# Gene products of two token tiles taken together: column groups shared by two tiles, and half of the array's rows for each tile's second product

## The chip, the cores and the metric

The kernel runs on one core of a Trainium2 chip. The metric is the device time of the whole program in microseconds, from a run of the core on the given inputs. Before the change three runs gave a median of 586.94 us (586.6 to 588.18).

## The reference

Two layers over x of 4 batches x 512 tokens x 256 features. Each layer normalises x and adds an attention-like part and a feed-forward part. The change lies in the feed-forward part of layer 0, which picks 32 of 512 "genes" for every token:

```python
logits = einsum('btd,gd->btg', xn, Wc) / clip(temperature, 0.1)
top_vals, top_idx = top_k(logits, 32)
expr_w = softmax(top_vals)
expressed = einsum('btk,btkc->btc', expr_w, genes[top_idx])     # 32 values a token
down = tanh(einsum('btc,dc->btd', expressed, Wd))
up = einsum('btc,dc->btd', expressed, Wu)
out = down * xn * up * scale
```

Beside it stands a linear attention with a running sum over the tokens. Layer 1 has another such attention (the "mixing"), a dense gated part, and 16 experts of which each token uses two.

## The kernel before

All is fp32. A tile is 128 tokens, a batch four tiles. The work runs in stages. In a stage the function `together` (L43) takes turns between generators: `layer0` (L224) of one batch or half batch, `mix` (L361) of the batch before it, and `dense` (L566), layer 1's dense part, a stretch of 11 chunks at a time, which has no other waits than its own and fills PE. The stages are L636 and L637 (batch 0 in two halves, so two tiles each), L643 to L645 (batches 1, 2 and 3 with four tiles each), and L673 on, where layer 0 is over. Then come routing, scatter, experts and the rest of the dense part. A scheduler puts the instructions of a stage in order on each engine, by what depends on what and in the order of the turns; each engine then runs its own list strictly from the front.

For one tile `layer0` does this. `logits` (L286) multiplies with Wc into a PSUM bank and ScalarE copies it out (L293). `top` (L296) is eight passes over 512 values on VectorE (L301, L302) and one product (L309) that leaves the unnormalised weights e of the 32 chosen genes, zero elsewhere, and the reciprocal rden of their sum. In between, a share of the attention is done (`attend_kv`, `attend_q`, L244 to L280). Then `express` (L313):

- four transposes turn e into one PSUM bank (L316), ScalarE copies it to wT (L318);
- four products with the genes, 128 rows and 32 columns each, one for each chunk of 128 genes (L321). Each writes 32 other partitions of one bank, so each lies in another column group of the array. The four partial sums are not added here: ScalarE copies all 128 partitions to exT (L322);
- one product of exT with wdut (L324) over 128 rows. wdut holds Wd and Wu side by side, repeated four times over the partitions (L126), so that this product adds the four partial sums too. Its 512 columns fill a bank;
- Tanh on ScalarE (L326), a small and a large product on VectorE (L328, L329), and on POOL four operations (L331 to L334) that put the result into xs.

After the tiles, `out` (L336) multiplies the attention with Wo, and VectorE adds it to xs (L342). In the next stage `mix` takes the statistics of xs. Its ScalarE part copies q and k (L391), takes squares (L396), a square root (L405, with a table load) and eight exponentials (L410, L411); its VectorE part has running sums (L421), a small softmax and top two for the router (L439 to L456). The dense part has pairs of products (L576), Tanh (L580), VectorE (L582), a copy (L586) and the products back (L596).

All layer 0 and mixing products take their PSUM bank from one pool of four (`bank`, L188). The tile pool of layer 0 (`io`) has two buffers of each name.

Of the kernel before, what the change touches and what calls it, by code (L numbers as in the profile page):

```python
# [11 lines left out]
F32 = mybir.dt.float32  # L12
# [4 lines left out]
P = 128  # L17
B, L, D = 4, 512, 256
NT = L // P
NH = D // P  # L20
NG, GD, NACT = 512, 32, 32
NGC = NG // P
# [31 lines left out]
def tile_two_layers(  # L54
# [24 lines left out]
    V, S, G, T = nc.vector, nc.scalar, nc.gpsimd, nc.tensor  # L79
# [41 lines left out]
    gn = wp.tile([P, NGC, GD], F32, name="gn")  # L121
    nc.sync.dma_start(gn, genes.rearrange("(c p) k -> p c k", p=P))

    wdut = wp.tile([P, 2 * D], F32, name="wdut")
# [60 lines left out]
    io = first.enter_context(tc.tile_pool(name="io0", bufs=2, side="right"))  # L185
    one = first.enter_context(tc.tile_pool(name="one0", bufs=1, side="right"))

    def bank():  # L188
        return ps_m.tile([P, L], F32, name="pm")
# [4 lines left out]
    def statistics(pool, b, i0, nt):  # L194

        mv = pool.tile([P, NT, 2], F32, name="mv")
        rs = pool.tile([P, 2, NT], F32, name="rs")
        ve = pool.tile([P, NT], F32, name="ve")
        for i in range(nt):
            bs = pool.tile([P, 6], F32, name="bs")  # L200
            V.bn_stats(bs, xs[:, b, i0 + i])
            V.bn_aggr(mv[:, i], bs)
        V.tensor_scalar(rs[:, 0, 0:nt], mv[:, 0:nt, 1], LN_EPS, None, ALU.add)
        V.reciprocal(ve[:, 0:nt], rs[:, 0, 0:nt])
        V.tensor_tensor(ve[:, 0:nt], ve[:, 0:nt], mv[:, 0:nt, 1], ALU.mult)
        V.tensor_scalar(rs[:, 1, 0:nt], ve[:, 0:nt], RMS_EPS, None, ALU.add)
        S.activation(rs[:, :, 0:nt], rs[:, :, 0:nt], AF.Sqrt)
        V.reciprocal(rs[:, :, 0:nt], rs[:, :, 0:nt])
        return mv, rs

    def normalise(to, b, i0, nt, mv, rs):
        for i in range(nt):
            V.tensor_scalar(
                to[:, i], xs[:, b, i0 + i], mv[:, i, 0:1], rs[:, 0, i : i + 1], ALU.subtract, ALU.mult
            )
# [8 lines left out]
    def layer0(b, i0, nt):  # L224

        W = nt * P
        mv, rs = statistics(io, b, i0, nt)
        xn = io.tile([P, NT, D], F32, name="xn")
        normalise(xn, b, i0, nt, mv, rs)

        sl = io.tile([P, 2, NT], F32, name="sl")
        V.tensor_scalar(sl[:, 0, 0:nt], rs[:, 1, 0:nt], rtemp, None, ALU.mult)
        V.tensor_scalar(sl[:, 1, 0:nt], rs[:, 1, 0:nt], scl, None, ALU.mult)
        yield
        xnT = io.tile([P, NH, L], F32, name="xnT")
        for h in range(NH):
            S.copy(xnT[:, h, 0:W], turn(xn, nt, h * P))
        yield


        def project(c):
            pm = bank()[:, 0:W]
            for h in range(NH):
                T.matmul(  # L244
                    pm,
                    wqkv[:, h, c * P : (c + 1) * P],
                    xnT[:, h, 0:W],
                    start=(h == 0),
                    stop=(h == NH - 1),
                )  # L250
            return pm

        def phi(c):

            pm = project(c)
            e = io.tile([P, L], F32, name="phi", bufs=3)[:, 0:W]
            S.activation(e, pm, AF.Relu, bias=nbqk[:, c : c + 1], scale=-1.0)
            S.activation(e, e, AF.Exp, scale=-1.0)
            V.scalar_tensor_tensor(e, pm, bqkv1[:, c : c + 1], e, ALU.add, ALU.max)
            return e  # L260

        ctxT = one.tile([P, NH, L], F32, name="ctxT")
        cums = {}

        def attend_kv(h):
            fk = phi(2 + h)
            pv = project(4 + h)
            kv = one.tile([P, L], F32, name="kv")[:, 0:W]
            V.scalar_tensor_tensor(kv, pv, bqkv[:, 4 + h : 5 + h], fk, ALU.add, ALU.mult)
            cum = io.tile([P, L], F32, name="cum")[:, 0:W]  # L270
            V.tensor_tensor_scan(
                cum, ones[:, 0:W], kv, carry[:, h : h + 1] if i0 else 0.0, ALU.mult, ALU.add
            )
            if i0 + nt < NT:
                V.tensor_copy(carry[:, h : h + 1], cum[:, W - 1 : W])
            cums[h] = cum

        def attend_q(h):
            fq = phi(h)
            V.scalar_tensor_tensor(ctxT[:, h, 0:W], fq, QSCALE, cums[h], ALU.mult, ALU.mult)  # L280


        rden = io.tile([P, NT], F32, name="rden")
        exT = one.tile([P, L], F32, name="exT")

        def logits(i):  # L286
            pl = bank()
            for h in range(NH):
                T.matmul(  # L289
                    pl, xnT[:, h, i * P : (i + 1) * P], wct[:, h], start=(h == 0), stop=(h == NH - 1)  # L290
                )
            lg = io.tile([P, NG], F32, name="lg")
            S.copy(lg, pl)  # L293
            return lg

        def top(i, lg):  # L296
            tp = io.tile([P, NACT], F32, name="top")
            rep = io.tile([P, NG], F32, name="rep")
            for r in range(NACT // 8):
                src = lg if r == 0 else rep  # L300
                V.max(tp[:, 8 * r : 8 * r + 8], src)  # L301
                V.match_replace(rep, tp[:, 8 * r : 8 * r + 8], src, TAKEN)  # L302
                if r == 0:
                    nm = io.tile([P, 1], F32, name="nm")
                    V.tensor_scalar(nm, tp[:, 0:1], sl[:, 0, i : i + 1], -1.0, ALU.mult, ALU.mult)
                    e = io.tile([P, NG], F32, name="e")
                    S.activation(e, lg, AF.Exp, bias=nm, scale=sl[:, 0, i : i + 1])
            den = io.tile([P, 1], F32, name="den")
            V.scalar_tensor_tensor(e, rep, TAKEN, e, ALU.is_equal, ALU.mult, accum_out=den)  # L309
            V.reciprocal(rden[:, i : i + 1], den)  # L310
            return e

        def express(i, e):  # L313
            pw = bank()
            for c in range(NGC):
                T.transpose(pw[:, c * P : (c + 1) * P], e[:, c * P : (c + 1) * P], ident)  # L316
            wT = io.tile([P, NGC, P], F32, name="wT")
            S.copy(wT.rearrange("p c t -> p (c t)"), pw)  # L318
            px = bank()
            for c in range(NGC):  # L320
                T.matmul(px[c * GD : (c + 1) * GD, 0:P], gn[:, c], wT[:, c], start=True, stop=True)  # L321
            S.copy(exT[:, i * P : (i + 1) * P], px[:, 0:P])  # L322
            du = bank()
            T.matmul(du, exT[:, i * P : (i + 1) * P], wdut, start=True, stop=True)  # L324
            dn = io.tile([P, D], F32, name="dn")
            S.activation(dn, du[:, 0:D], AF.Tanh, scale=rden[:, i : i + 1])  # L326
            cf = io.tile([P, 1], F32, name="cf")
            V.tensor_tensor(cf, rden[:, i : i + 1], sl[:, 1, i : i + 1], ALU.mult)  # L328
            V.scalar_tensor_tensor(dn, du[:, D : 2 * D], cf, dn, ALU.mult, ALU.mult)  # L329
            xw = io.tile([P, D], F32, name="xw")  # L330
            G.tensor_tensor(xw, xn[:, i], nwb, ALU.mult)  # L331
            G.tensor_tensor(dn, dn, xw, ALU.mult)
            G.tensor_tensor(xs[:, b, i0 + i], xs[:, b, i0 + i], bob, ALU.add)
            G.tensor_tensor(xs[:, b, i0 + i], xs[:, b, i0 + i], dn, ALU.add)  # L334

        def out(i):  # L336
            ao = bank()[:, 0:D]
            for h in range(NH):
                T.matmul(  # L339
                    ao, ctxT[:, h, i * P : (i + 1) * P], wot[:, h], start=(h == 0), stop=(h == NH - 1)  # L340
                )
            V.tensor_tensor(xs[:, b, i0 + i], ao, xs[:, b, i0 + i], ALU.add)  # L342


        parts = [lambda h=h, f=f: f(h) for h in range(NH) for f in (attend_kv, attend_q)]
        lg = logits(0)
        for i in range(nt):
            nxt = logits(i + 1) if i + 1 < nt else None
            e = top(i, lg)
            yield  # L350
            for part in parts[i * len(parts) // nt : (i + 1) * len(parts) // nt]:
                part()
            yield
            express(i, e)
            lg = nxt
            yield
        for i in range(nt):
            out(i)
            yield
# [270 lines left out]
    def a(b, i0, nt):  # L630
        return layer0(b, i0, nt), 2 + 4 * nt
# [170 lines left out]
    for step, _ in enumerate(dd):  # L802
# [11 lines left out]
        while added < 2 * NTT and 17 * added <= 32 * (step - 3):  # L814
# [4 lines left out]
            if added % 4 == 0 and added < 2 * NTT:  # L819
                b, i = divmod(n - 1, NT)  # L820
# [55 lines left out]
```

## Time and profile before

| | |
|---|---|
| runs, median (lowest to highest) | 586.94 us (586.6 to 588.18) |
| the profiled execution | 591.42 us |
| its span, first to last instruction | 589.7 us |
| mean granted TensorE clock | 0.975 |
| busy: PE, weight loads, DVE, ACT, POOL | 539.4, 393.0, 373.1, 232.6, 173.9 us |
| L321, 128 passes on PE | 7.0 us busy, 293 ns each |
| L324, 32 passes on PE | 17.8 us busy, 639 ns each |
| L318 and L322, 16 copies each on ACT | 9.2 and 4.2 us |
| L301 and L302, 64 each on DVE | 43.9 and 43.2 us |

PE is TensorE's products, DVE VectorE, ACT ScalarE, POOL GpSimd. Busy time of PE counts each pass to its modelled end, and passes overlap: a pass of 512 columns is listed with 592 ns, yet the next one starts 0.43 us later. So the starts, not the lengths, tell what a product costs. The chain of waits is followed back from the last instruction: for each step, what released it.

### The profile page before, as it was taken

What the parts mean: (1) busy time and instruction counts of PE and PEld (TensorE: products, weight loads), DVE (VectorE), ACT (ScalarE), POOL (GpSimd) and SP (SyncE); (2) the same over time, 40 slices, a digit from 0 to 9 for tenths busy, and PEclk for the clock granted to TensorE, in tenths of its full rate; (3) what the DMA queues carried; (4) which work ended last, traced back from release to release, by engine and by line L of the source; (5) the groups of instructions that cost most, each with busy time, mean ns of one, the idle gap of its engine ahead of it and who ended that gap; (6) DMA issues with size and microseconds to landing.
All of it is one profiled execution on the core that took longest, in us unless ns stands there. A gap on an engine that the chain in (4) does not pass through costs nothing.

```text
span 589.7 us, 7350 instructions
## 1 busy us (share of the span) xinstructions
PE 539.4 (91%) x2384; PEld 393.0 (67%) x2384; DVE 373.1 (63%) x992; ACT 232.6 (39%) x528; POOL 173.9 (29%) x214
## 2 busy tenths in 40 slices
PE   3557989989999999999999999969999999999987
PEld 1334656558565685656877778857777777788876
DVE  3979999997896797967943785322222222235563
ACT  1453746653555625556265311103333333321111
POOL 1234232353221432224440326661000000006651
PEclk9788999999999999999999999989999999999999
DMA  4993000000000000000075602224233333114441
GB/s 159 375 377 140 1 1 1 2 0 1 1 1 0 1 1 1 1 1 1 1 236 170 182 2 80 91 86 136 90 108 107 108 108 98 55 63 125 126 133 46
DMA packets 38453, 47.39 MB, mean 80 GB/s; under 512 B 4016, under 2 KB 34960, under 8 KB 38160
## 3 DMA queue, kind: packets, MB, share of 16 engines
q1 hardware_dynamic: 35344, 38.53, 20.0%
q0 software_dynamic: 3072, 8.39, 4.6%
q8 instruction: 20, 0.33, 0.2%
q14 instruction: 17, 0.14, 0.1%
HBM read 28.30 MB, written 18.61 MB: 80 GB/s over the span
## 4 chain that ended last, share of the span: by engine, by line
PE 61%; DVE 21%; ACT 6%; POOL 4%; issue 3%; DMA 2%; SPq 0%; another core or an unknown queue 0%; POOLq 0%; ACTq 0%; DVEq 0%
PE gu L576 16%; PE pu L740 9%; PE acc L596 9%; PE py L761 7%; PE pm L384 5%; DVE rep L302 4%; DVE top L301 4%; PE pt L703 3%; POOL xrows L544 3%; PE pm L244 3%; PE pm L289 2%; PE pm L221 2%; PE pm L339 2%; DVE sums L430 2%; DVE sums L421 1%
## 5 line engine op out<-in xcount | busy, mean ns | idle before, releaser
L576 PE MATMUL gu<-yT,wugt 128*128 128x256 f32 x512 | 127.5, 385 | 0.0
L576 PEld LDWEIGHTS gu<-yT,wugt 128*128 128x128 f32 x512 | 96.0, 192 | 19.5 <-issue 7.2
L580 ACT ACTIVATE th<-gu 128x256 f32<-128x256 f32 (+1 forms) x88 | 33.0, 382 | 133.4 <-PE gu L576 85.9
L806 POOL DMA_INDIRECT ys<-yrows,slot x32 | 30.7, 961 | 145.4 <-PE gu L576 130.1
L596 PE MATMUL acc<-wot,hid 128*128 128x256 f32 x256 | 67.4, 386 | 5.9 <-DVE hid L584 5.5
L582 DVE SCALAR_TENSOR_TENSOR th<-th,gu 128x256 f32<-128x256 f32 (+1 forms) x88 | 36.1, 412 | 55.0 <-ACT th L580 46.3
L740 PE MATMUL pu<-wex,xgT 128*128 x188 | 63.8, 461 | 0.8 <-DMA xg<-xrows 0.8
L587 POOL TENSOR_TENSOR hid<-hid,th 128x256 f32<-128x256 f32 (+1 forms) x44 | 34.3, 782 | 101.1 <-ACT hid L586 97.8
L596 PEld LDWEIGHTS acc<-wot,hid 128*128 128x128 f32 x256 | 48.4, 192 | 15.5 <-DVE hid L584 5.9
L244 PE MATMUL pm<-xnT,wqkv 128*128 128x512 f32 (+1 forms) x120 | 46.7, 529 | 4.1 <-ACT lg L293 1.8
L576 PE MATMUL gu<-xn1T,sgu 128*128 128x256 f32 (+1 forms) x192 | 47.3, 382 | 1.4 <-ACT hid L586 1.3
L749 DVE TENSOR_TENSOR hb<-pu,hb 128x176 f32<-128x176 f32 x47 | 16.1, 342 | 51.0 <-ACT hb L748 51.0
L384 PE MATMUL pm<-w,xn1T 128*128 128x512 f32 (+1 forms) x128 | 45.7, 501 | 0.0
L761 PE MATMUL py<-wex,hgT 128*128 x188 | 44.5, 379 | 0.0
L761 PEld LDWEIGHTS py<-wex,hgT 128*128 128x128 f32 x188 | 35.6, 190 | 8.6 <-issue 0.2
L576 PEld LDWEIGHTS gu<-xn1T,sgu 128*128 128x128 f32 (+1 forms) x192 | 33.8, 181 | 9.5 <-ACT hid L586 2.6
L740 PEld LDWEIGHTS pu<-wex,xgT 128*128 128x128 f32 x188 | 32.0, 190 | 11.0 <-ACT xgT L717 1.0
L384 PEld LDWEIGHTS pm<-w,xn1T 128*128 128x128 f32 x128 | 24.6, 193 | 21.4 <-issue 17.9
L244 PEld LDWEIGHTS pm<-xnT,wqkv 128*128 128x128 f32 x120 | 23.8, 202 | 22.0 <-issue 13.2
L753 DVE COPY hgT<-pt 128x512 f32<-128x512 f32 (+1 forms) x24 | 16.3, 681 | 34.2 <-PE pt L703 34.2
L544 POOL DMA_INDIRECT xrows<-xn,slot x32 | 31.0, 969 | 23.8 <-DVE cpair L538 9.9
L301 DVE MAX8 top<-rep 128x8 f32<-128x512 f32 x48 | 32.9, 686 | 0.4
(162 smaller groups left out, 881.5 us busy)
## 6 DMA issues: line engine op xcount, KB each, us to landing
xrows<-zero SPq DMA_DIRECT2D x1, 6016.0 KB, 22.6
xg<-xrows SPq DMA_DIRECT2D x23, 256.0 KB, 2.7
yrows<-yg SPq DMA_DIRECT2D x23, 256.0 KB, 2.1
wex<-in_w_gate_up_dram SPq DMA_DIRECT2D x8, 704.0 KB, 4.8
xs<-in_x_dram SPq DMA_DIRECT2D x4, 512.0 KB, 7.7
wugt<-in_wug_dram SPq DMA_DIRECT2D x1, 2048.0 KB, 12.3
wex<-in_w_down_dram SPq DMA_DIRECT2D x4, 512.0 KB
out_dram<-xs SPq DMA_DIRECT2D x7, 256.0 KB, 2.7
```

What stands on the lines that cost most here:

```text
L244: T.matmul(pm, wqkv[:, h, c * P : (c + 1) * P], xnT[:, h, 0:W], start=(h == 0), stop=(h == NH - 1),)
L301: V.max(tp[:, 8 * r : 8 * r + 8], src)
L384: T.matmul(o[:, 0:n], xnT[:, h, i * P : (i + 1) * P], w1[:, h, at : at + n], start=(h == 0), stop=(h == NH - 1),)
L544: sc = G.indirect_dma_start(out=xrows, out_offset=bass.IndirectOffsetOnAxis(ap=slot[:, k, i : i + 1], axis=0), in_=xn1[:, i // NT, i % NT] ...
L576: T.matmul(gu[0:m, k], w[:, h, at : at + m], ins[which][:, h], start=(h == 0), stop=(h == NH - 1))
L580: S.activation(th[0:m], gu[0:m, 0], AF.Tanh, scale=0.5)
L582: V.scalar_tensor_tensor(th[0:m], th[0:m], 1.0, gu[0:m, 0], ALU.add, ALU.mult)
L587: G.tensor_tensor(hid[0:m], hid[0:m], th[0:m], ALU.mult)
L596: mm = T.matmul(acc[:, t], hid[0:m, t * P : (t + 1) * P], dw[0:m, dc], start=(n == 0 and t == 0), stop=(n == NC - 1), skip_group_check=True,)
L740: T.matmul(pg[:, 0 : 2 * NI], xT[:, i, h], wex[:, bass.ds(at[i] + h * 2 * NI, 2 * NI)], start=(h == 0), stop=(h == NH - 1),)
L761: mm = T.matmul(py[:, i * D : (i + 1) * D], hT[:, i, h], wex[:, bass.ds(at[i] + EW - (2 - h) * D, D)], start=(h == 0), stop=(h == 1),)
L806: G.indirect_dma_start(out=ys[:, asked], out_offset=None, in_=yrows, in_offset=bass.IndirectOffsetOnAxis(ap=slot[:, k, n : n + 1], axis=0) ...
```

## The change

`express` is split. `turn_genes` keeps the transposes and the copy to wT. A tile's wT is kept until the next tile has its own; then one `express` serves both tiles:

- the four column groups hold two tiles, two groups each. A tile's four chunks of 128 genes go into its two groups, two chunks added up in each. These are eight products for two tiles, as before;
- one copy of 128 partitions to exT for both tiles: the lower 64 belong to the first, the upper 64 to the second;
- the second product of each tile takes 64 rows, the lower or the upper half of the array, into a bank of its own;
- the rest, now `expressed`, is done for one tile and then the other.

```diff
-        exT = one.tile([P, L], F32, name="exT")
...
-        def express(i, e):
+        def turn_genes(e):
             pw = bank()
             for c in range(NGC):
                 T.transpose(pw[:, c * P : (c + 1) * P], e[:, c * P : (c + 1) * P], ident)
             wT = io.tile([P, NGC, P], F32, name="wT")
             S.copy(wT.rearrange("p c t -> p (c t)"), pw)
+            return wT
+
+        def express(i, wTs):
             px = bank()
-            for c in range(NGC):
-                T.matmul(px[c * GD : (c + 1) * GD, 0:P], gn[:, c], wT[:, c], start=True, stop=True)
-            S.copy(exT[:, i * P : (i + 1) * P], px[:, 0:P])
-            du = bank()
-            T.matmul(du, exT[:, i * P : (i + 1) * P], wdut, start=True, stop=True)
+            for c in range(2):
+                for g in range(NGC):
+                    j = g % 2 * 2 + c
+                    T.matmul(
+                        px[g * GD : (g + 1) * GD, 0:P], gn[:, j], wTs[g // 2][:, j], start=(c == 0), stop=(c == 1)
+                    )
+            exT = io.tile([P, P], F32, name="exT")
+            S.copy(exT, px[:, 0:P])
+            dus = [bank(), bank()]
+            for t, du in enumerate(dus):
+                half = slice(t * P // 2, (t + 1) * P // 2)
+                T.matmul(du, exT[half], wdut[half], start=True, stop=True)
+            for t, du in enumerate(dus):
+                expressed(i + t, du)
+
+        def expressed(i, du):
             dn = io.tile([P, D], F32, name="dn")
...
         lg = logits(0)
+        wTs = []
         for i in range(nt):
             nxt = logits(i + 1) if i + 1 < nt else None
             e = top(i, lg)
...
-            express(i, e)
+            wTs.append(turn_genes(e))
+            if len(wTs) == 2:
+                express(i - 1, wTs)
+                wTs = []
             lg = nxt
             yield
```

In the changed kernel's numbering the transposes are L315, the copy L317, the first products L327, exT L331, the second products L335, Tanh L341, and L595 is the dense L576.

## The prediction

> **What bounds the kernel now.** I read the page's row of slices first, then the busy time by stage, then the chain of waits from 250 us, then single instructions around the gene products. The first stages last until about 290 us; a 75 us stage is one batch of four tiles, with dense chunks as filler.
>
> Slices of the page (14.7 us each) and the stage 215 to 290 us (columns: window and length, then busy time and count by engine):
>
> ```profile
> PE   3557989989999999999999999969999999999987
> DVE  3979999997896797967943785322222222235563
> ...
> 215.00:290.00 75.00, 72.51 (x317) 48.50 (x316) 63.31 (x161) 39.77 (x89) 21.88 (x26) 1.00 0.00 1
> ```
>
> PE is busy 72.5 of 75 us, DVE 63.3. Until 90 us DVE is the full one (39.6 of 40 us from 50 to 90); after 290 us the edit touches nothing. But who ends last changes inside the stage. The chain (start, length, what):
>
> ```profile
> 250.42 0.34 DVE th L582
> ...
> 251.16 0.50 ACT wT L318
> 251.66 0.04 issue
> 251.70 0.43 PE pm L321 x8
> 252.13 0.63 PE gu L576 x2
> 252.76 0.88 PE pm L324 x2
> ...
> 261.92 1.73 PE pm L244 x4
> 263.65 0.02 issue
> 263.67 0.69 ACT phi L257
> ...
> 270.04 0.15 ACT exT L322
> ...
> 271.85 0.47 ACT dn L326
> ...
> 273.03 0.42 DVE th L582
> ...
> 275.67 1.14 DVE sums L421
> 276.81 0.04 issue
> 276.86 0.66 PE pm L316 x4
> ```
>
> So: VectorE from 223 to 251 us (the top-32 search, no gap over 0.15 us between 227 and 253), PE to 263.7, ScalarE to 273, VectorE to 276.8, then PE to the next batch. From this a saved PE microsecond counts only between 251.7 and 263.7 and after 276.8. The last two lines say why PE stood idle 1.37 us at 275.4: the transposes of tile 3's e wait for a PSUM bank that the scan frees.
>
> Now the edited products themselves, for one tile (start, busy):
>
> ```profile
> 251.70 0.43 PE L321 MATMUL pm<-wT,gn 128*32 128x128 f32 x8
> ...
> 252.06 0.70 PE L576 MATMUL gu<-yT,wugt 128*128 128x256 f32 x2
> ...
> 252.59 1.04 PE L324 MATMUL pm<-wdut,exT 128*128 128x512 f32 x2
> ```
>
> An fp32 product is two passes here. The eight passes of L321 in four column groups start at 251.70 and the next full-array pass at 252.06: 0.36 us, where two passes of 128 columns one after the other take 0.21 (L289 streams 512 columns in 0.43, so 128 take 0.107). So the four groups do run side by side, and 0.15 us goes to draining. The pair behind is 0.70 us busy instead of the usual 0.59: 0.1 more, weights that could not be loaded ahead.
>
> **What the skill says.** "TensorEngine Tiling (Array Packing)", Key Properties: tiles work independently, but changing the tiling mode drains the array; the 0.15 + 0.1 us above agree. "TensorE: Matmul & The Clock Gate", Part 3, Measured speedup: row groups overlap like column groups, 4 tiles of K=32, N=512 gave 3.07 times. No row group appears in this trace; the column groups agree in kind. The same page, Part 3, What overlaps: matmuls start and end in program order. Whether that holds up the second tile behind the first tile's second fp32 pass, no run here shows. "TensorEngine Tiling", Gotcha 1: row tiles need different PSUM banks; the edit takes two.
>
> **The change, part by part.**
>
> *1. First product.* Still eight passes per tile. Before, a tile costs 0.36 + 0.10 = 0.46 us of PE. After, a pair in one piece is 4 x 0.107 + 0.25 = 0.68. But the changed program's instruction order splits it in five of eight pairs: the first tile's two products, a dense product, the other six. That is 0.46 + 0.68 = 1.14 against 0.92 before. The first two wait for nothing new and lie in the wait for wT.
>
> *2. Second product.* Before 2 x 0.438 (mean slot of L324 from start to next start) = 0.88 per tile, 1.75 per pair. After, if both row groups overlap fully, 2 x 0.427 = 0.85, plus a drain 0.15 and weights exposed before and after, 0.1 to 0.2: 1.15. Bounds: 0.95 (everything hidden); 1.55 if only the middle passes overlap (3 x 0.427 + 0.25); 2.05 to 2.5 with no overlap (1.75 + 0.3, or each load exposed too). I take 1.15: the column groups in fp32 show full overlap and use the same hardware.
>
> *3. Copies.* One exT copy (0.27 us, 0.15 on the chain) per pair goes. Two Tanh (0.47 each), two products with cf (0.47), and their POOL work stay, in a burst at the second tile.
>
> *4. What moves.* The even tile's products leave their place. What that gives, stage by stage:
>
> Stage 215 to 290. (a) One dn (0.47 busy, 0.39 on the chain) leaves the full VectorE run: -0.4 at wT. PE's 1.3 us for the even tile leave that run too, and buy nothing: PE just waits longer for wT. (b) From wT to the first mixing products: before 251.70 to 253.64 = 1.94; after 0.68 + 0.43 + 1.15 = 2.26, so +0.3; and one dense pair of passes now stands behind instead of ahead, +0.4. At 263.7 that is -0.4 + 0.3 + 0.4 = +0.3. (c) In ScalarE's run the third tile's exT and dn go, 0.27 + 0.47: -0.4 at the last exp. (d) At 273 the router's small operations (L445 to L455, 2.2 us) stand ahead of the scan. In the changed order the router's Exp comes ahead of phi's, so they can run during ScalarE's eight exps. From the end of phi's Exp (267.8) VectorE still has 0.65 phi, 0.41 th, 0.74 kv, 0.3 small, 1.21 cum, 0.71 replace, 0.66 chosen = 4.7, until 272.5; then th 0.42 and the scan 1.14, until 274.1; 0.6 more for gaps and the later start: 274.7 instead of 276.8, -2.1 at L316. PE can follow: of the way there it was idle 1.37, and tile 2's products (1.34) are gone. (e) Last pair: before 276.86 to the out products at 281.54; after, 0.68 + 1.15 against one tile's 1.34, +0.5. Stage: **-1.6**.
>
> Stage 140 to 215: same order, but VectorE had a 0.51 us gap at 168.6 where PE was late, and the even tile's products lie in PE's own stretch; so (a) is -0.4 - 0.5 = -0.9, the rest as above: **-2.1**.
>
> Stage 90 to 140: VectorE is full but for 0.85 us at 103.9, where logits wait behind tile 0's products; that goes, -0.8, and a dn, -0.4; the last pair costs +0.5: **-0.7**.
>
> 50 to 90: VectorE full, its work unchanged. The two tiles' POOL work (0.73 + 1.3 each) now comes in one burst before the sums of L342: **+0.3**, bounds 0 and +1. It is hidden later: with four tiles POOL ended at 286 and the out sums are at 291.
>
> Start: the six projections of the second half waited behind tile 0's products, 25.1 to 28.7 us; VectorE has 3 us of idle there, but POOL still adds the tiles one by one: **-0.5**, bounds -1.5 and +1 (PE's clock was 0.79 here, and longer gaps may keep it low).
>
> Waits added: tile 1's bank. PE stops there with dense work queued behind it; four banks turn over, the pair holds px and then two. I take 0 and bound it by the longest wait PE had for a bank, 1.5 us per stage at worst.
>
> Sum: -0.5 + 0.3 - 0.7 - 2.1 - 1.6 = **-4.6 us**. The profiled execution took 591.42, its span 589.7 and 1.7 around; it would give 586.8. The median of the runs is 4.5 us lower than this execution. I apply the difference as it is: 586.94 - 4.6 = **582.3 us**.
>
> **Rivals.**
> *Absorbed.* (c) and (d) do not come, since PE or another ScalarE wait is late next. For it: PE is 97% busy, and only 1.37 us were idle. Then stages 4 and 5 give about -0.5 each: -0.5 + 0.3 - 0.7 - 1.0 = -1.9, and with partial overlap (1.55) back some 1 to 2 us: **586.0**.
> *Slower: the row tiles run one after the other.* Two fp32 passes of tile 0 go first in order, tile 1's behind them, and each half loads its weights exposed. A pair then takes 2.3 (between 2.05 and 2.5), 1.15 more, in about seven pairs that lie on PE's path: +8.0 - 4.6 = +3.4, **590.4**. For it: no row tile in the trace, and each half has its own semaphore. Against: the column groups overlap in the same two passes. It decides from 2.05 us per pair on: (2.05 - 1.15) x 7 = 6.3, which is the 4.6 gained and 1.8 more.
> *The change isn't what it says*: the order keeps pairs but the dense products between them force full-array mode each time. That is in the 1.14 above; for all eight pairs it adds 3 x 0.46 = 1.4: 583.7.
>
> **How the numbers follow.** Forecast with its last variant 0.55, absorbed 0.23, slower 0.22. A difference under 0.3% (1.8 us) cannot be told from none. The forecast is faster, up to its low end: a pair at 0.95 saves 8 x 0.2 = 1.6, the start another 1: 579.5. Absorbed lies from 584 to 587.5, half of it within 0.3%, a third faster; the serial case from 588 to 591.5, mostly slower. Range 579.5 to 590: it leaves out the tail of the serial case. Faster 0.59, same 0.19, slower 0.22.
>
> **What would show it.** Right: L335's four passes start in two waves 0.43 us apart and the next full-array pass 1.0 to 1.2 us after the first; PE idle before the last pair's transposes (1.37 us) shrinks; the stages get 1.5 to 2 us shorter each. Wrong: four starts 0.43 us apart (no overlap), or PE waits on L335 for VectorE (bank). Wrong in (d) if the scan still starts 3 us after the last exp. A stage that stays 75 us long with a PE that idles more is "absorbed".

## The result, and the profile after

Six runs of each kernel gave a median of 587.06 us before (586.12 to 588.18) and **583.53 us** after (582.32 to 585.08): a ratio of 0.9943, 95% interval 0.9928 to 0.9958, so 3.4 us faster. The profiled execution after took 584.1 us, its span is 582.3 us, the mean granted clock 0.981.

The two profiled spans differ by 7.4 us, more than the timed 3.4: from the first to the last scatter the kernel before took 43.9 us and the changed one 39.4. Over all profiles this length goes with the chip and not with the edit: about 44 us on the two chips on which the kernel before took 591 us, 39.4 on the two on which it took 587, for single products (even_twice below) and paired ones alike. It would also explain why the profiled execution before was 4.5 us above its median. I therefore compare stretches that end before the scatter, and timed runs.

The page's slices after, 14.6 us each; PE is at eight tenths or more from about 58 us on, but for two slices:

```profile
PE   3637989989999999999999989997999999999997
DVE  3969999998896897968943686331222222225563
```

And the stage from 215 to 290 us (window and length, then busy time and count of PE, weight loads, DVE, ACT, POOL):

```profile
215.00:290.00 75.00, 73.55 (x325) 49.66 (x324) 63.95 (x167) 39.65 (x88) 22.47 (x27) 1.00 0.00 1
```

In a fixed window PE is 1.0 us busier, though each pair now takes less of it: the stage has become shorter and more of the next work falls into the window (325 passes instead of 317). So a busy sum over a fixed window says nothing here; places in the stage have to be compared.

The chain of waits after, same stage (start, length, what):

```profile
247.25 0.34 DVE th L601
...
247.98 0.50 ACT wT L317
...
248.52 0.63 PE pm L327 x12
249.15 0.63 PE gu L595 x2
249.78 1.06 PE pm L335 x4
250.84 2.83 PE pm L403 x8
...
270.52 0.45 PE pm L221 x4
...
270.99 1.23 DVE sums L440
```

Before, ScalarE was on this chain from 263.7 to 273 us and VectorE to 276.8. Now PE is on it all the way from 248.5 to 271 us, and only the scan (L440) stands between that and tile 3's transpositions. Those single instructions, PE only (start, busy, and in brackets the idle time before and what ended it), first the transposition before the change and then the changed kernel:

```profile
276.86 0.33 PE L316 MATMUL pm<-ident,e 128*128 128x128 f32 x1 [1.21 <-DVE sums L421]
```

```profile
272.27 0.66 PE L315 MATMUL pm<-ident,e 128*128 128x128 f32 x4 [0.44 <-DVE sums L440]
...
273.73 0.50 PE L327 MATMUL pm<-wT,gn 128*32 128x128 f32 x8
274.16 0.70 PE L595 MATMUL gu<-yT,wugt 128*128 128x256 f32 x2
274.79 1.13 PE L335 MATMUL pm<-wdut,exT 64*128 64x512 f32 x4
275.85 1.13 PE L595 MATMUL gu<-yT,wugt 128*128 128x256 f32 x4
```

The idle time before the transpositions fell from 1.21 to 0.44 us. The four passes of L335 occupy PE from 274.79 to 275.85, 1.06 us for two tiles. In the single records they start at 274.790, 274.797, 275.323 and 275.330: two waves 0.53 us apart, both row tiles within 7 ns. The dense pass ahead of them is followed after 0.31 us instead of the usual 0.22 (both from the single records), so a pair takes 0.09 us more than its own 1.06. PE never waited on L335 for a bank; its only wait there is ScalarE's exT.

Where in the stage the time went. All are starts on PE after the stage's start, which I set at the end of the last addition of `out` (L342, L357 after) of the batch before (the last mixing ends with its last yT); stage 140 to 215 us:

| us from the stage's start | before | changed | same rows | delay only | router first | four together |
|---|---|---|---|---|---|---|
| tile 1's transpositions | 32.36 | 30.56 | 30.56 | 30.56 | 32.36 | 30.56 |
| first mixing product behind them | 35.53 | 34.71 | 35.57 | 35.47 | 35.53 | 31.00 |
| tile 2's transpositions | 49.84 | 49.54 | 50.41 | 49.77 | 49.83 | 46.60 |
| tile 3's transpositions | 58.92 | 56.20 | 57.07 | 56.71 | 57.99 | 53.53 |
| first `out` product | 63.44 | 61.61 | 63.33 | 62.70 | 62.51 | 61.60 |
| end | 75.20 | 73.18 | 74.05 | 73.87 | 74.26 | 75.18 |

The stage after it shows the same differences within 0.3 us (0.6 with four together), but for some ends. The last four columns are experiments. And the lengths of all stages, from the same ends:

| kernel | stage 2 (two tiles) | 3 | 4 | 5 | 6 (last mixing) |
|---|---|---|---|---|---|
| before | 44.5 | 59.0 | 75.2 | 75.1 | 49.8 |
| changed | 43.5 | 59.7 | 73.2 | 73.5 | 50.8 |
| same rows | 43.5 | 60.1 | 74.1 | 74.1 | 51.4 |
| delay only | 43.9 | 58.7 | 73.9 | 76.6 | 49.4 |
| router first, in the kernel before | 44.0 | 60.4 | 74.2 | 74.2 | 49.6 |
| router first, in the changed kernel | 43.6 | 60.3 | 73.9 | 74.1 | 50.3 |
| one piece | 42.8 | 58.9 | 73.2 | 75.7 | 49.4 |
| even tiles' product twice | 43.6 | 62.1 | 76.1 | 75.9 | 49.8 |
| stage 3 single | 43.7 | 60.6 | 73.2 | 73.2 | 50.8 |
| batch 0 single | 44.2 | 64.0 | 73.2 | 73.2 | 50.8 |
| four together | 43.3 | 62.7 | 75.2 | 74.5 | 53.6 |

### The profile page after: what moved, and what is told of

It reads as the page before. It is cut to its first block, busy times and chain, and to the rows that moved or that the text cites. A ratio compares the mean times of both kernels' runs of the same rounds, so it can differ in the third digit from the quotient of the medians.

```text
span 582.3 us, 7339 instructions
## 1 busy us (share of the span) xinstructions
PE 535.6 (92%) x2384; PEld 391.5 (67%) x2384; DVE 371.6 (64%) x992; ACT 231.4 (40%) x520; POOL 169.6 (29%) x214
## 4 chain that ended last, share of the span: by engine, by line
PE 51%; DVE 28%; POOL 7%; issue 6%; ACT 4%; DMA 4%; SPq 0%; POOLq 0%; ACTq 0%; DVEq 0%
PE gu L595 11%; PE pu L759 10%; PE py L780 7%; PE acc L615 6%; DVE rep L301 5%; DVE top L300 5%; PE pm L403 4%; PE pt L722 4%; POOL ys L825 3%; DVE sums L449 3%; POOL xrows L563 2%; DVE sums L440 2%; PE pm L244 2%; PE pm L221 2%; PE pm L288 2%
## 5 line engine op out<-in xcount | busy, mean ns | idle before, releaser
L595 PE MATMUL gu<-yT,wugt 128*128 128x256 f32 x512 | 125.4, 382 | 0.0
L595 PEld LDWEIGHTS gu<-yT,wugt 128*128 128x128 f32 x512 | 95.0, 190 | 20.4 <-issue 8.8
L615 PE MATMUL acc<-wot,hid 128*128 128x256 f32 x256 | 66.0, 381 | 0.4
L759 PE MATMUL pu<-wex,xgT 128*128 x188 | 65.1, 468 | 0.8 <-ACT xgT L736 0.8
L601 DVE SCALAR_TENSOR_TENSOR th<-th,gu 128x256 f32<-128x256 f32 (+1 forms) x88 | 36.6, 417 | 44.0 <-ACT th L599 43.7
L606 POOL TENSOR_TENSOR hid<-hid,th 128x256 f32<-128x256 f32 (+1 forms) x44 | 33.1, 756 | 101.9 <-ACT hid L605 96.0
L595 PE MATMUL gu<-xn1T,sgu 128*128 128x256 f32 (+1 forms) x192 | 46.9, 381 | 1.4 <-ACT hid L605 1.3
L780 PE MATMUL py<-wex,hgT 128*128 x188 | 44.5, 379 | 0.0
L595 PEld LDWEIGHTS gu<-xn1T,sgu 128*128 128x128 f32 (+1 forms) x192 | 34.0, 182 | 9.5 <-ACT hid L605 2.6
L605 ACT COPY hid<-gu 128x256 f32<-128x256 f32 (+1 forms) x44 | 16.4, 373 | 43.1 <-DVE th L601 42.9
```

The source lines that it names most:

```text
L595: T.matmul(gu[0:m, k], w[:, h, at : at + m], ins[which][:, h], start=(h == 0), stop=(h == NH - 1))
L601: V.scalar_tensor_tensor(th[0:m], th[0:m], 1.0, gu[0:m, 0], ALU.add, ALU.mult)
L606: G.tensor_tensor(hid[0:m], hid[0:m], th[0:m], ALU.mult)
L615: mm = T.matmul(acc[:, t], hid[0:m, t * P : (t + 1) * P], dw[0:m, dc], start=(n == 0 and t == 0), stop=(n == NC - 1), skip_group_check=True,)
L759: T.matmul(pg[:, 0 : 2 * NI], xT[:, i, h], wex[:, bass.ds(at[i] + h * 2 * NI, 2 * NI)], start=(h == 0), stop=(h == NH - 1),)
L780: mm = T.matmul(py[:, i * D : (i + 1) * D], hT[:, i, h], wex[:, bass.ds(at[i] + EW - (2 - h) * D, D)], start=(h == 0), stop=(h == 1),)
```

## The experiments

Each kernel was timed in five rounds beside the kernel before on the same chip; a ratio is to that.

**Does the overlap make the gain? (same_rows)** The changed kernel, with both second products on the lower 64 rows, so that they cannot lie side by side.

```diff
-            exT = io.tile([P, P], F32, name="exT")
-            S.copy(exT, px[:, 0:P])
+            exT = io.tile([P // 2, 2, P], F32, name="exT")
+            for t in range(2):
+                S.copy(exT[:, t], px[t * P // 2 : (t + 1) * P // 2, 0:P])
...
-                T.matmul(du, exT[half], wdut[half], start=True, stop=True)
+                T.matmul(du, exT[:, t], wdut[0 : P // 2], start=True, stop=True)
```

> The changed kernel, but both second products of a pair take the lower 64 rows (the second tile's half is copied down; one small copy more a pair), so that they cannot overlap; order on the engines nearly the same. Theory (the pairs lie in stretches where the array is late, and only the overlap pays for the pairing): a pair takes 1.95 us instead of 1.06, in six to seven of eight pairs on the path, +5.5 to +6.5: about 589.5 us, above the kernel before. Rival (the gain comes from the even tile's work leaving its place and from the new order of the router's operations, array time is hidden): within 1.5 us of the changed kernel, about 584.5.

Measured 1.0005 (0.9990 to 1.0019). PE in the trace of this kernel:

```profile
201.51 1.98 PE L335 MATMUL pm<-wdut,exT 64*128 64x512 f32 x4
203.42 1.13 PE L595 MATMUL gu<-yT,wugt 128*128 128x256 f32 x4
```

From start to next start 1.91 us instead of 1.06. In the table each pair puts this kernel 0.86 us further behind the changed one, 1.72 at the first `out` product. That is the array time alone: the second exT copy, which this kernel has besides, adds nothing at these places. So with both products on the same rows nothing of the gain is left, and the overlap is worth 0.62% of 587 us, 3.6 us against these. That lies between the 5.5 to 6.5 us of the theory and the 1.5 of the rival. The saved array time itself is larger: summed over stages 2 to 5, second products take 7.4 us in the changed kernel and 13.4 here. About 0.6 of a saved microsecond arrives at the end (0.4 to 0.8 by the intervals of the two ratios); the stage's end already shows 0.87 of the 1.72.

**Is the gain in the later place alone? (delay_only)** The kernel before, each tile with its own products as before, but both done at the second tile.

```diff
-            express(i, e)
+            wTs.append(turn_genes(e))
+            if len(wTs) == 2:
+                express(i - 1, wTs[0])
+                express(i, wTs[1])
+                wTs = []
```

> The kernel before, with its own products (four column groups and 128 rows for each tile), but both tiles' products stand at the second tile. Theory: the delay without the overlap puts an even tile's 1.3 us into the array's stretches and takes less than that from the others: 586 to 589 us, no gain. Rival (the delay is the gain): 583.5.

Measured 0.9979 (0.9966 to 0.9993): 1.2 us faster, a third of the gain. The table shows its way: tile 1's transpositions come 1.8 us earlier, which the first mixing product loses again (35.47 against 35.53), tile 3's come 2.2 us earlier, of which the last pair's products give back 1.5. The later place lets things start earlier; the overlap keeps the bill small. The other two thirds, about 2 us, come with the rest of the edit, the products that overlap.

**Is it the router's place? (before_router, after_router)** The router's largest value, Exp, sum and reciprocal written ahead of the square root in `mix`, once in each kernel.

```diff
+        V.tensor_reduce(mx, lg, AX.X, ALU.max)
...
+        S.activation(ee[:, :, 0:NE], ee[:, :, 0:NE], AF.Exp)
...
+        V.reciprocal(den, den)
         cf = w2.tile([P, 2, NT], F32, name="cf1")
```

> The kernel before, with the first half of the router's work (maximum, Exp, sum, product) written ahead of the square root of the mixing, nothing else changed. Theory (the router's small operations ahead of the scan held up the array 2 us in each of two stages): -2 to -4 us, 583 to 585. Rival (the change gained by array time alone; this order is worth nothing): 586.5 to 587.5.

> The changed kernel with the same edit of the router. Theory (the changed kernel's order already has this): within 1.5 us of the changed kernel, 582.5 to 585. Rival (the two add up): 580.

Measured 0.9985 (0.9968 to 1.0001) in the kernel before, whose chain now reads:

```profile
274.64 1.23 DVE sums L432
...
275.92 0.66 PE pm L316 x4
```

The wait for the scan ahead of tile 3's transpositions is 0.4 us instead of 1.2, and they come 0.93 us earlier in both late stages. So the small router operations did hold the scan back, and are worth 0.9 us in each late stage; stage 3 grew by 1.4 us and took most of it back. The 2 to 4 us of the theory did not come: the interval reaches from -1.9 us to none. In the changed kernel, measured 0.9996 (0.9981 to 1.0010), the same edit loses 3 us: the router's Exp is ahead already, and the new order puts tile 3's transpositions 1.0 us later. Neither theory had that; why this order is worse was not followed further.

**Control, and the split first products (after_again, one_piece)** The changed kernel unaltered, and with its eight first products held together by an order without a wait:

```diff
-                for g in range(NGC):
+                for g in (2, 3, 0, 1):
...
+                        tc.add_manual_dep(
+                            mm.ins,
+                            lead,
+                            mybir.DependencyInfo(mybir.DependencyClass.NoSync, mybir.DependencyReason.DATA),
```

> The changed kernel again, beside the others on one chip. Theory: ratio to the kernel before 0.993 to 0.996, as measured first. Rival (part of the first difference came from the chip): 0.997 or more.

> The changed kernel, with the eight first products of a pair held together in the array's order (the second tile's first), so that no dense product splits them. Theory (the split pair's first two products lie in the wait for the second tile's copy, and buy and cost nothing): within 1 us of the changed kernel, ratio to it 0.998 to 1.002. Rival (each split costs 0.46 us of array time on the path): 2 us faster, 0.9965.

Measured 0.9946 (0.9925 to 0.9967) and 0.9940 (0.9918 to 0.9963). From its first start to the next full-array start a pair's first products take 0.57 us, instead of 0.34 and 0.56 in two pieces, and the whole gains nothing that can be told. In stages 4 and 5 the reason is in the trace: behind the early piece PE waits 0.3 us for wT in any case.

**What is a microsecond of PE worth at each tile? (even_twice, odd_twice)** The kernel before, with the second product of the even (or odd) tiles done twice into the same bank: eight times 0.86 us, 6.9 us of array time.

```diff
-            T.matmul(du, exT[:, i * P : (i + 1) * P], wdut, start=True, stop=True)
+            for _ in range(2 if i % 2 == 0 else 1):
+                T.matmul(du, exT[:, i * P : (i + 1) * P], wdut, start=True, stop=True)
```

> The kernel before, with the second product of every even tile done twice: 8 times 0.86 us more on the array. Theory (most even tiles lie where VectorE or ScalarE is last, and the array waits): +1 to +2 us of the 6.9. Rival (the array is 97% busy and every microsecond counts): +6 to +7 us.

> The kernel before, with the second product of every odd tile done twice: again 8 times 0.86 us. Theory (odd tiles lie in the array's own stretches): +5 to +6 us. Rival (every place is alike): the same as with the even tiles.

Measured 1.0119 (1.0097 to 1.0141) and 1.0165 (1.0143 to 1.0187): 7.2 and 10.5 us more. The theory that the even tile's time is free fell. Stages 4 and 5 took 0.8 to 0.9 us of the 1.72 added there for even tiles and 1.2 to 1.5 for odd ones. In stage 4 the even tiles are not alike: tile 0's second product puts tile 1's transpositions 0.86 us later, all of it, and tile 2's adds less than 0.1 at tile 3's. Stage 3 took 3.1 and 3.7, more than was added, so it answers to more than the amount of its array time.

**Stage 3 (single_b1, single_b0)** The changed kernel, with one tile at a time in stage 3 alone, and in the two stages of batch 0 alone.

```diff
+            if b == 1:
+                express_one(i, wTs.pop())
```

> The changed kernel, but the third stage (batch 1, about 90 to 143 us) keeps the products of one tile at a time, as before the change. In the changed kernel's trace that stage was 0.8 us longer than before although TensorE was busy 1.2 us less in it. Theory, the stage loses because both tiles' results come late and together and VectorE's run to the end of the stage is met: this kernel gets the 0.8 us back, the stage is about 51.4 us as a difference from 53 or so (as long as in the kernel before within 0.4 us), and the whole is 0.5 to 1.0 us faster than the changed kernel, a ratio of about 0.993 to the kernel before. Rival, the stage lost for another reason (its start, or the order in which the next stage's work is let in) and the saved 1.4 us of array time are paid back later: the whole is 0.5 to 1.5 us slower than the changed kernel, a ratio of 0.996 to 0.997.

> The changed kernel, but the two stages of two tiles (batch 0, to about 83 us) keep the products of one tile at a time; the three stages of four tiles stay paired. It is the counterpart of the kernel whose third stage alone was left single, in which that stage stayed long (60.6 us) and TensorE still stood idle for about 0.75 us at its start. Theory, the third stage loses by what the pairing before it does to the order of work handed over at its start: here the idle time at its start is gone and the stage is 59 us or less (59.7 in the changed kernel), while the second stage is back at 44.3 to 44.7 us (43.5), so that the whole is within 0.8 us of the changed kernel, a ratio of 0.993 to 0.996. Rival, the third stage is set by VectorE, which is busy in all but 3 us of it whatever is paired: the stage stays at 59.5 us or more, the second stage's gain is lost, and the whole is about 1 us slower than the changed kernel, a ratio of 0.996 to 0.997.

single_b1: 0.9956 (0.9942 to 0.9970), by the ratios 0.8 us slower than the changed kernel, though the two intervals overlap; in the trace stage 3 lasts 60.6 us, 0.9 more than in the changed kernel, and the later stages are alike. The stage has the same products as in the kernel before and is 1.6 us longer. So pairing inside stage 3 gained 0.9 us, as the rival said, and pairing in batch 0, before it, costs this stage more than that.

single_b0: 1.0046 (1.0031 to 1.0060), 5.9 us slower than the changed kernel, 4.4 of it in stage 3 (64.0 us), whose products are those of the changed kernel. Both theories missed this size, and the two effects do not add: pairing in batch 0 alone makes the stage 1.6 us longer than before, in stage 3 alone 5.1, both together 0.7. What DVE and PE waited for in it (in total, times, longest):

```profile
DVE xn L213 <- POOL xw L356: 2.4, 1, 2.4
```

```profile
PE pm L221 <- DVE phi L259: 4.0, 1, 4.0
```

and its chain of waits:

```profile
112.36 0.68 POOL xw L356
113.05 0.68 POOL dn L357
...
114.49 0.74 POOL xw L356
...
115.25 0.41 DVE xn L213
...
123.49 0.66 DVE phi L259
...
124.19 0.69 PE pm L221 x2
...
126.16 2.56 PE gu L607 x6
```

The xn (L213) is that of batch 3. With two buffers it goes where batch 1's xn lies, and may not be written until POOL has read that one for its last tile (xw). An xw is made two tiles ahead, so tile 3's stands on POOL's list behind dn and xs of both tiles of the first pair. DVE's list is strictly in order and has xn there, so DVE stands 2.4 us, the feature map phi (L259) comes late behind it, and PE waits 4.0 us. A second loss follows: in this trace the granted TensorE clock, as a share of full speed, is 0.50 from 122.0 to 128.8 us, where the changed kernel has 1.00 through the whole stage, and six dense passes take 2.56 us instead of 1.30. By estimate, 4.6 us of work at half the clock (124.2 to 128.8) lose 2.3 us; PE's idle time in the stage is 2.9 us above the changed kernel's. In the changed kernel a part of the search stands ahead of xn on DVE and fills this wait. DVE is nearly the bound in this stage: from 84 to 143 us it is busy 57.2 of 59 us in the changed kernel (before: 56.5). Over these kernels stage 3 lasts from 58.7 to 64.0 us without following the array time. Part of the longest times is the clock; the rest I put down to the order of the lists, DVE's above all, but only single_b0's wait was followed.

**More overlap (quad, quad_s1)** All four tiles of a stage together: one column group each, second products on 32 rows each; quad_s1 with stage 3 single.

```diff
-            for c in range(2):
+            for c in range(m):
                 for g in range(NGC):
-                    j = g % 2 * 2 + c
+                    j = g % n * m + c
...
-            if len(wTs) == 2:
-                express(i - 1, wTs)
+            if len(wTs) == nt:
+                express(0, wTs)
```

> The changed kernel, with all four tiles of a four-tile stage in one set of first products (a column group each, four chunks added up in it) and four second products on 32 rows each. TensorE's time for the second products should fall from 2.12 us for four tiles to between 1.1 (all four side by side) and 2.1 us (no further overlap), in three stages. Theory, array time counts at about 0.6 and the tail of the stage is unchanged: 1 to 2 us faster than the changed kernel, a ratio of 0.991 to 0.993. Rival, four results at once, with four banks held and ScalarE's, VectorE's and GpSimd's work of four tiles in one burst behind the last tile, cost more than the array time is worth: 1 us or more slower than the changed kernel, a ratio of 0.996 or above, with the time from the last tile's first transposition to the first output product grown from 5.6 us to 7 or more.

> Both edits: four tiles together in the last two four-tile stages, one tile at a time in the third stage. If what each edit is worth stands by itself, the ratio is the product of the two: ratio of single_b1 times what four tiles together gained or lost in the last two stages alone. Theory: 1 to 2 us faster than the changed kernel, ratio 0.991 to 0.993. Rival, the burst of four costs more than it saves: slower than single_b1 by 0.5 us or more.

Measured 1.0102 (1.0087 to 1.0117) and 1.0055 (1.0034 to 1.0077): the rival held, 9 and 6.5 us slower than the changed kernel. PE in quad, stage 3 and stage 4:

```profile
125.85 1.14 PE L337 MATMUL pm<-wdut,exT 32*128 32x512 f32 x8
126.92 0.70 PE L597 MATMUL gu<-yT,wugt 128*128 128x256 f32 x2
```

```profile
202.21 1.14 PE L337 MATMUL pm<-wdut,exT 32*128 32x512 f32 x6
...
205.74 1.12 PE L337 MATMUL pm<-wdut,exT 32*128 32x512 f32 x2 [0.90 <-DVE sums L442]
```

Four row tiles cost what two do, 1.07 us. In stages 4 and 5 only three go together; the fourth needs a fourth bank, comes 3.5 us later (the last 0.90 a wait for DVE to free one), and behind it PE waits another 1.9 us a stage for dn (L346), which reads these banks. PE's idle time is 3.8 us in each of these stages, against 1.1 and 1.5 in the changed kernel, and the saving is gone. Tile 3's transpositions come 2.7 us earlier than in the changed kernel and the first `out` product at the same time, 8.1 us later instead of 5.4. Then the chain of quad at 280 us runs over POOL:

```profile
280.67 1.11 POOL dn L349
...
281.86 0.72 POOL xs L351
282.58 0.69 POOL xw L348
283.27 0.69 POOL dn L349
```

With four tiles' results in one burst behind the last tile, the stage ends 13.6 us after the first `out` product instead of 11.6. In stage 3 the burst meets the wait of single_b0 again, POOL's xw ahead of batch 3's xn, with the same second loss:

```profile
132.50 1.60 DVE xn L213 x2
134.09 0.40 DVE dn L346
134.50 0.04 issue
134.54 2.07 PE pm L356 x4
```

PE stood 3.3 us before these four passes, the granted clock is 0.50 from 131.3 to 138.1 us, and they take 2.07 us, where four of the same at full clock take 0.86. So a part of the 9 us is the clock and not the banks or POOL. No version I tried beats the changed kernel beyond the uncertainty of the runs.

## Why the prediction was right, and where it was not

The time came to 583.5 against 582.3 forecast, and the mechanism in stages 4 and 5 was the forecast one. By its steps:

- **Second product (2).** Forecast 1.15 us a pair; measured 1.06 from its first start, and 0.09 on the pass ahead of it: the row tiles overlap fully. The waves are 0.53 us apart, not 0.43 as the sign was given. The serial rival fell with that; same_rows, which has its condition, came to +0.3 us against the +3.4 that it was priced at, so that rival was also priced too high: it charged every pair in full to the path and took 2.3 us for a pair that measured 1.91 (2.00 with the pass ahead). "TensorE: Matmul & The Clock Gate", Part 3, What overlaps, left open whether the order of starts holds up the second tile; here it does not.
- **First product (1).** Forecast 1.14 us split and 0.68 in one piece, draining and exposed weights included. Measured from first start to the next full-array start 0.34 + 0.56 and 0.57, with 0.10 more on the pass behind each piece: 1.1 and 0.68. That the split costs nothing that can be told, one_piece shows.
- **Banks.** Taken as 0, and right for two tiles. With four together the wait appeared, 0.9 us in each late stage for the fourth bank.
- **Stage 4 and 5.** Forecast -2.1 and -1.6, measured -2.0 and -1.6. Inside, (a) with (b) gave -0.7 to -0.8 at the first mixing product against -0.6 and -0.1: the clause that PE's 1.3 us for the even tile "buy nothing" failed. Delaying the pair puts tile 1's transpositions 1.5 to 1.8 us earlier, and even_twice shows that tile 0's PE time is on the path in full. (c) and (d) were right in sum, -2.7 and -2.6 at tile 3's transpositions against -2.6 and -2.1; the router's part alone is 0.9 in the kernel before (before_router), and that the rest is tile 2's products leaving is by subtraction, not shown. (e) was mis-sized: the last pair costs +0.9 instead of +0.5 (5.41 us from transpositions to `out` against 4.52). In stage 5 this cancels with what the other steps gave too little, so that its end agrees better than its parts.
- **Start.** Forecast -0.5, not to be told: the first stage ended at 39.7 and 38.5 us in two profiles of the changed kernel and at 39.4 in that of the kernel before, and the time at a granted clock of 0.5 between 20 and 32 us was 6.9, 3.4 and 10.3 us in them.
- **Stage 2.** Forecast +0.3, measured -1.0. The step counted only POOL's burst; tile 1's transpositions came 1.9 us earlier (33.29 against 35.14 after the stage's start).
- **Stage 3, wrong in sign.** Forecast -0.7, measured +0.7. The gain that the step named came: tile 1's transpositions are at 22.49 us of the stage instead of 24.36. Tile 2's are at 36.02 instead of 35.30, tile 3's at 43.45 instead of 44.49. Then the last pair: from tile 3's transpositions to the first `out` product 6.78 us instead of 5.14, so +1.6 where the sum had +0.5, and this alone is 1.1 of the 1.4 us. The chain of the changed kernel there:

```profile
128.91 0.37 ACT hid L605
129.28 0.53 ACT phi L258
129.81 0.17 ACT exT L331
...
130.02 1.13 PE pm L335 x4
```

  The pair's exT (a copy) stands on ScalarE behind a hid and a phi of the dense part and the attention, which come late from the full VectorE; with single tiles (single_b1) the same way takes 4.92 us. What costs tile 2 its 0.7 us is not settled.
- **Missing from the sum: stage 6.** That "after 290 us the edit touches nothing" failed: the last mixing takes 50.8 us instead of 49.8, with 0.4 us more idle time on PE. Stages 5 and 6 together gain 0.6 of stage 5's 1.6 us. In one_piece the border lies elsewhere (75.7 and 49.4), with the same time of the whole program: dense work moved over the border (95 passes of L604 in stage 5 instead of 88 of L595).

Forecast in all -4.6, timed -3.4. The 1.2 us between are near what stage 3 (+1.4 off) and stage 6 (+1.0) took and stage 2 (-1.3) gave. That the total came so close is in part luck: the gain of stage 2, for which the step gave no reason, made up for nearly all that stage 3 lost. (The range's low end is 0.2 us off in its own sum: 582.3 - 1.6 - 1 is 579.7.)

## What to carry to other kernels

Two products that leave half of the array's rows idle each can share it, and where dense work fills the rest, some 0.6 of the saved array time arrived in this kernel; a test that keeps the edit and forbids the overlap tells that share. Ask for what else the grouping bundles: two results at once were carried, four at once met the number of banks and POOL's burst. When a variant is slower than its waits explain, read the granted clock of that stretch: a wait on PE was followed by slower passes in two kernels here. Where VectorE is full, price an order as uncertain by a microsecond or more rather than forecast a few tenths.

## What the runs showed of the hardware

- fp32 row tiles of 64 rows start within 7 ns of each other (in seven of eight pairs; in the first pair, after an idle time, 0.10 us), and the second wave 0.53 us after the first, not the 0.43 of full-array passes. Two products on the same rows have 0.53, 0.43, 0.43 and 0.52 us between starts, so about 0.1 is added once at each end of the group, and 0.09 on the pass ahead. A pair costs 1.06 us without that pass, against 1.91 for the same two products on the same rows and 1.75 before, so halving the rows saves nothing by itself.
- Four row tiles of 32 rows cost 1.07 us, against 4 x 0.875 = 3.5 for whole-array products: 3.3 times (3.0 with the 0.09 of the pass ahead), near the 3.07 that "TensorE: Matmul & The Clock Gate", Part 3, Measured speedup, states for four such tiles.
- In stage 3 the granted clock is 1.00 throughout in all kernels but two. In single_b0 PE stood 4.0 us and in quad 3.3 us at a stretch there, and both show 6.8 us at 0.50, which began during the wait and outlasted it by 4.6 and 3.6 us.
- An added 1.72 us of PE work made one stage 3.7 us longer, at full clock (odd_twice, stage 3): a stage can return more than was put in. Why was not followed.
